# Where tiles of a shared PSUM ring stand beside a grouped-product unit, in a message-passing kernel on one core

## The chip, the cores and the metric

The kernel runs on one core of a Trainium2 chip. The metric is the device time of one execution in microseconds (us); lower is better. The engines are named as in the profile: PE (matrix products; PEld are its weight loads), DVE (vector engine), ACT (scalar engine), POOL (GpSimd) and SP, whose queue issues most DMAs.

## The reference

Cut to what matters (200000 edges, 6250 nodes, 128 features, 20 edge attributes):

```python
h = relu(layernorm(x)) @ W_in                                  # 6250 x 128
W_ij = (ssp(f_ij @ W_f1 + b_f1) @ W_f2 + b_f2) * cutoff        # 200000 x 128
out = segment_sum(h[idx_j] * W_ij, idx_i, num_segments=6250)   # scatter-add over the edges
return x + ssp(out @ W_o1 + b_o1) @ W_o2 + b_o2                # ssp(v) = softplus(v) - log 2
```

`idx_j` (dst) is sorted, and is drawn as 6250 times the square of a uniform number; `idx_i` (src) is random. So the gather walks slowly through the table of nodes, and the sum scatters to all of it.

## The kernel before

Edges are taken in chunks of 128 and quads of 512; there are 391 quads (`NQ`), and two quads make one load (`load_sc`). One long Python loop over iterations `i` writes the order of every engine by hand (`tc.manual_schedule`), as a pipeline in software: iteration `i` loads ahead, computes the first layer of quad `i` (tiles `z`, `e`, one-hot `oh`, then the guard `a`, L314), gathers and multiplies quad `i-1` (`xg`, `W`, `xc`, then the product `m`, L344), and sums and scatters quad `i-2`.

Sums over equal source nodes go two ways.

- A *plain* quad builds an equality matrix of its 128 source ids for each chunk (`s1_eq`, tile `eq`, L308, one iteration after its one-hot), multiplies with it on PE (`s3_pe`, tile `pp`, L356), copies (ACT, L364), and POOL scatters four chunks with an indirect DMA into one of four accumulators in DRAM (L399).
- A *sorted* quad (144 of them, `mpq` = 5, 8, 10, 13, 16, 18, ..., three in every 8 iterations) is permuted on chip instead: a rank of each edge within its group of nodes, one-hots `pm` (L484), products `pq` (L508), copies `mst` (L516). Each six sorted quads make a round, and a round is summed into the accumulator `accT` in SBUF in four **grouped-product units**. A unit has six one-hots on DVE (`unit_oh`, tile `so`, L583, one iteration ahead), 72 products on PE into four PSUM tiles (`unit_pe`, tiles `un`, L598), and four additions on DVE (`unit_evac`, L607 in the first round, else L609, one iteration later). There are 96 units. Up to the last four they stand in iterations 23, 26, 31, 34, 39, 42, ...: where `i` modulo 8 is 7 or 2.

Besides, `rank_group`, `rank_count` (PSUM tile `rkp`), `rank_own`, `rank_over` (`rko`) and `rank_slot` rank eight sorted quads at a time (18 groups); `prep_*` fills the node table for 256 nodes at a time (PSUM tiles `hps`, `xps`, to iteration 217); `over_row` and `over_sum` (`orow`, `osum`) gather the edges that overflow a group; `r0_load`, `r0_tp`, `r0_add` (`r0t`, `rtp`) add the first DRAM accumulator to `accT` in 13 pieces once it is complete, from iteration 373 on; `late_bias` (`bps`) folds two biases once.

There are two PSUM rings of four banks. The first, "A", holds `z`, `xg` and `W`. The second, "B", holds all the rest: `pp`, `pq`, `po`, `un`, `rkp`, `rko`, `orow`, `osum`, `hps`, `xps`, `rtp`, `bps`. Tiles take the banks of a ring in turn, so a tile waits for the last reader of the one four places ahead of it. A unit takes all four banks at once, and its products go round over the four tiles.

The order of one iteration (each `run` carries out what was put at that point; in a point, what was registered first goes first: prep, bias, `r0`, ranks, the sorted quads' own steps, units):

```python
run(i, "L"); run(i, "A0"); run(i, "D0")      # loads; ACT copies; DVE reads of last iteration's tiles
s3_idx(i - 3); s1_oh(i); s1_eq(i - 1)        # DVE
run(i, "D1")                                 # DVE
s2_pe_x(i - 1); s2_pe_w(i - 1); s1_pe(i + 1) # PE: xg, W, z
s1_exp(i); s1_ln(i); run(i, "A1"); s2_copy(i - 1)   # ACT
s1_guard(i); s2_m(i - 1)                     # DVE: a (L314), m or pt (L344)
s3_pe(i - 2); s3_copy(i - 2, 0); s3_copy(i - 2, 1)  # PE pp; ACT s
run(i, "PE2"); run(i, "A2"); run(i, "D2")    # PE: ring B; ACT; DVE: pm, so, pt
s3_scatter(i - 3); run(i, "S")               # POOL
```

In the iteration of a unit, `i-2` is a sorted quad and no `pq` or `po` is due, so PE's part of ring B holds the unit alone, with what else was put at "PE2" ahead of it. The buffers of tag `pm` (two) serve both the one-hots `pm` and the tiles `r0t`. After the loop comes a tail of 13 groups: it loads the other three accumulators from DRAM, adds `accT`, and applies the last two layers.

Of the kernel before, what the change touches and what calls it, by code (L numbers as in the profile page):

```python
# [30 lines left out]
RND = 6  # L31
RKQ = 8
PW = 386
PREP_GAP = 9
# [8 lines left out]
def tile_gnn(ctx: ExitStack, tc: tile.TileContext, x, fB, cT, srcT, srcr, dstr, win_, wf1, wf2, bias, bo1c, wo1,  # L43
# [11 lines left out]
    spread = big(NSC)  # L55
    NCH = -(-n_edges // P)
    NQ = -(-NCH // 4)
# [3 lines left out]
    NG = len(groups)  # L61
# [6 lines left out]
    GN = NP // GRP  # L68
    mpq = sorted_quads(NQ)
    mpi = {q: n for n, q in enumerate(mpq)}  # L70
    plain = {q: n for n, q in enumerate(q for q in range(NQ) if q not in mpi)}
    scat = [0] * (NQ + 12)
    for q in range(NQ):
        if q not in mpi:
            scat[q + 3] += min(4, NCH - 4 * q)
    for q in mpq[1::2]:
        scat[q + 9] += 1
    RET = max(120, sum(scat) - 64)
    ret_at = min(i for i in range(len(scat)) if sum(scat[:i + 1]) >= RET)

# [177 lines left out]
    def load_sc(s):  # L258
        n = min(SC, NQ * SEG - s * SC)
        pp, hh, nh = s % HALF, s // HALF, n // SEG  # L260
        top = caps[s]
        ft = fts[s % len(fts)]
        b, o = s * SC // BE, s * SC % BE
        nc.sync.dma_start(ft[:KF, :n], fsd[b].rearrange("g (r e) -> (g r) e", r=RB)[:, o:o + n])
        sb = ld.tile([P, SC], I16, tag="sb", name="sb")
        nc.sync.dma_start(sb[:, :n], src16[s:s + 1, :n].to_broadcast([P, n]))
        rb = ld.tile([NR, SC], BF16, tag="rb", name="rb")
        nc.sync.dma_start(rb[:, :n], reld[s:s + 1, :n].to_broadcast([NR, n]))
        wn = ld.tile([NR, 2, P], BF16, tag="wn", name="wn")
        _, regs = nc.values_load_multi_w_load_instructions(  # L270
            base_i[pp:pp + 1, hh, 0:nh], engines=[SP], min_val=0, max_val=top,
            skip_runtime_bounds_check_because="clamped on the chip to [0, top]")
        for j in range(nh):
            nc.sync.dma_start(wn[:, j, :], tab[bass.ds(regs[j] * 3, NR), :])
        loads[s] = (ft, sb, rb, wn)

    def s1_pe(q):
        ft = loads[q // 2][0]
        j = q % 2
        z = ps.tile([P, 512], F32, tag="A", name="z", bufs=4)  # L280
        nc.tensor.matmul(z, ws, ft[:K1, j * SEG:(j + 1) * SEG], start=True, stop=True)  # L281
        st.setdefault(q, {})["z"] = z
# [12 lines left out]
    def s1_oh(q):  # L295
        rb = loads[q // 2][2]
        j = q % 2
        oh = wk.tile([NR, 512], BF16, tag="oh", name="oh")
        nc.vector.tensor_scalar(oh, rb[:, j * SEG:(j + 1) * SEG], rowid[:NR], None, op0=ALU.is_equal)  # L299
# [342 lines left out]
    with tc.manual_schedule():  # L642
# [107 lines left out]
        def at(i, point, fn, *a):  # L750
            hooks.setdefault((i, point), []).append((fn, a))

        def run(i, point):
            for fn, a in hooks.pop((i, point), []):
                fn(*a)
# [57 lines left out]
            at(t0 + 1, "A1", fb_3, b)  # L813
            at(t0 + 1, "D2", fb_4, b)

        mid = NQ // 6 * 3 if spread else 0

        def late_loads():
            nc.sync.dma_start(bo2b, bias[1:2, :].to_broadcast([P, P]))
# [43 lines left out]
        for t in range(0, NPT, 4):  # L863
            i = mid + 8 * (t // 4) if spread else 0
            at(min(i + 9, NQ + 1), "D2", x_bias, t)
        for g in range(len(tgroups)):
            i = ret_at + 3 + g
            at(min(i, NQ + 2), "L", r0_load, g)
            at(min(i + 2, NQ + 3), "PE2", r0_tp, g)
            at(min(i + 3, NQ + 4), "D0", r0_add, g)  # L870
        for r in range(-(-len(mpq) // RKQ)):
            i = mpq[RKQ * r]
            at(i - 4, "D2", rank_group, r)
            at(i - 3, "PE2", rank_count, r)
            at(i - 2, "D0", rank_own, r)
            at(i - 1, "PE2", rank_over, r)
            at(i, "D0", rank_slot, r)
        for q in mpq:
            at(q + 1, "D2", perm_oh, q)
            at(q + 2, "D2", part_rem, q, 1)  # L880
            at(q + 2, "D2", part_rem, q, 2)
            for s in range(4):
                at(q + 3 + s // 2, "PE2", permute, q, s)
                at(q + 4 + s // 2, "A0", perm_out, q, s)
            at(q + 4, "D1", perm_loc, q, 0)
            at(q + 5, "D1", perm_loc, q, 1)
            at(q + 4, "PE2", over_pe, q)
            at(q + 5, "A0", over_out, q)
            if mpi[q] % 2:
                at(q + 5, "D2", over_idx, q)  # L890
                at(q + 6, "PE2", over_row, q)
                at(q + 7, "D0", over_eq, q)
                at(q + 8, "PE2", over_sum, q)
                at(q + 9, "A0", over_copy, q)
                at(q + 9, "D1", over_ji, q)
                at(q + 9, "S", over_scatter, q)
        last = mpq[-1]
        for r in range(len(mpq) // RND):
            nxt = [mpq[n] + 2 for n in range(RND * (r + 1), min(RND * (r + 2), len(mpq))) if mpq[n] - mpq[n - 1] == 3]
            for s in range(4):  # L900
                k = nxt[s] if nxt else last + 6 + 2 * s
# [5 lines left out]
        for i in range(max(NQ + 6, last + 14)):  # L907
# [12 lines left out]
            if 0 <= i - 1 < NQ:  # L920
                s2_pe_x(i - 1)
                s2_pe_w(i - 1)
            if i + 1 < NQ:
                s1_pe(i + 1)
            if i < NQ:
                s1_exp(i)
                s1_ln(i)
            run(i, "A1")
            if 0 <= i - 1 < NQ:
                s2_copy(i - 1)  # L930
            if i < NQ:
# [12 lines left out]
            run(i, "S")  # L944
# [17 lines left out]
    with tc.For_i(0, trips, 1) as ci:  # L962
# [47 lines left out]
        s = wk.tile([P, P], F32, bufs=1, tag="dg", name="fs")  # L1010
# [112 lines left out]
def sorted_quads(nq):  # L1123
    qs, q = [], MP0
    while q < nq - MPEND:
        qs.append(q)
        q += MPGAPS[(len(qs) - 1) % len(MPGAPS)]
    return qs[:len(qs) // RND * RND]


def runs(qs):
# [109 lines left out]
```

## Time and profile before

| | |
|---|---|
| runs | 2337.44, 2331.75, 2336.96 us; median 2336.96 us |
| profiled execution | 2332.85 us; its span, first to last instruction, 2331.0 us |
| mean granted TensorE clock | 0.948 |
| busy, share of the span | PE 86%, DVE 84%, POOL 74%, ACT 73% |
| last scatter issued | 2272.3 us, then the tail |

A row of the profile's groups reads: line, engine, operation, tiles written <- read, times it occurs | busy us, mean ns of one | idle time of the engine just before it, and what ended most of that. A row of the waits reads: who waited <- for whom: us in total, times, longest. A row of the timeline reads: start, duration (several alike merged, xN), and in brackets the idle time before it and what ended that. A row of the windows gives a stretch, its length, each engine's busy time, and the granted clock.

### The profile page before, as it was taken

How to read it: one execution, taken by the hardware profiler on the slowest of the kernel's cores; microseconds unless marked ns; L12 is line 12 of the kernel's file. 1: busy time of each engine (PE TensorE's matmuls, PEld its weight loads, DVE VectorE, ACT ScalarE, POOL GpSimd, SP SyncE). 2: the span in 40 equal slices, each digit the busy share in tenths (PEclk: the TensorE clock that was granted, in tenths of full speed). 3: DMA queues.
4: the chain of work that ended last, by engine and by line, in shares of the span. 5: the costliest groups of instructions: out<-in, count | busy, mean ns of one | idle time of the engine just before them, and what ended most of it. 6: DMA issues, size and time to landing. Idle time of an engine off the chain costs nothing.

```text
span 2331.0 us, 55463 instructions
## 1 busy us (share of the span) xinstructions
PE 2009.1 (86%) x19201; PEld 1405.5 (60%) x19201; DVE 1946.9 (84%) x5586; ACT 1706.7 (73%) x4286; POOL 1728.0 (74%) x1101
## 2 busy tenths in 40 slices
PE   4878988888889888989898989898989898987775
PEld 3556655666656565656565656665666565664543
DVE  6778988888889888879898989898989898886565
ACT  4777877786778776868787878786878787875534
POOL 3678778776768676768677888787878787886464
PEclk8899999999999999999999999999999999998888
DMA  8977768676767676767766767776767676776438
GB/s 295 246 167 138 155 126 164 118 154 119 152 126 157 136 145 121 148 136 144 146 136 140 160 119 157 143 148 130 150 136 148 137 156 121 148 154 136 98 34 223
DMA packets 391004, 341.76 MB, mean 147 GB/s; under 512 B 86760, under 2 KB 305742, under 8 KB 390720
## 3 DMA queue, kind: packets, MB, share of 16 engines
q1 hardware_dynamic: 237136, 265.37, 38.0%
q0 software_dynamic: 153296, 72.75, 32.0%
q8 instruction: 151, 2.47, 0.4%
q14 instruction: 133, 1.09, 0.2%
q10 hardware_dynamic: 288, 0.07, 0.0%
HBM read 198.15 MB, written 139.90 MB: 145 GB/s over the span
## 4 chain that ended last, share of the span: by engine, by line
PE 45%; DVE 30%; ACT 11%; DMA 6%; issue 5%; SPq 1%; POOL 1%; DVEq 0%; ACTq 0%; POOLq 0%
PE pq L508 10%; PE un L598 10%; PE W L333 8%; PE pp L356 6%; DMA acc<-s,ji 4%; DVE so L583 4%; DVE pm L484 4%; ACT xc L339 3%; DVE pt L498 3%; DVE a L314 3%; PE W L330 2%; PE xg L325 2%; DVE eq L308 2%; DVE m L344 2%; ACT e L287 2%
## 5 line engine op out<-in xcount | busy, mean ns | idle before, releaser
L399 POOL DMA_INDIRECT acc<-s,ji x987 | 1573.9, 1595 | 526.4 <-issue 170.5
L339 ACT ACTIVATE xc<-xg,cT_sb 128x128 f32<-128x128 f32 x1564 | 440.4, 362 | 268.0 <-PE xg L325 258.7
L598 PE MATMUL un<-so,mst 32*128 32x392 bf16 x6912 | 381.1, 365 | 186.2 <-DVE pr L448 56.6
L508 PE MATMUL pq<-pt,pm 128*128 128x386 bf16 x2304 | 452.5, 335 | 27.7 <-ACT s L364 15.2
L333 PE MATMUL W<-w,a 128*128 128x128 f32 x3128 | 460.4, 291 | 0.0
L333 PEld LDWEIGHTS W<-w,a 128*128 128x128 f32 x3128 | 385.0, 194 | 95.7 <-issue 95.3
L598 PEld LDWEIGHTS <-mst 32*128 32x128 bf16 x6912 | 206.8, 103 | 344.4 <-issue 159.4
L516 ACT CAST mst<-pq 128x386 bf16<-128x386 f32 x576 | 271.8, 500 | 95.9 <-PE pq L508 79.5
L508 PEld LDWEIGHTS <-pm 128*128 128x128 bf16 x2304 | 223.5, 98 | 180.5 <-issue 37.7
L314 DVE SCALAR_TENSOR_TENSOR a<-z,e 128x512 f32<-128x512 f32 x391 | 267.4, 684 | 70.4 <-ACT e L292 43.4
L292 ACT ACTIVATE e<-e,con 128x512 f32<-128x512 f32 x391 | 282.2, 722 | 12.7
L609 DVE TENSOR_TENSOR accT<-un,accT 128x392 f32<-128x392 f32 x368 | 182.2, 557 | 125.8 <-PE un L598 113.1
L356 PEld LDWEIGHTS pp<-m,eq 128*128 128x128 f32 x1976 | 262.3, 194 | 37.0 <-DVE accT L609 24.6
L356 PE MATMUL pp<-m,eq 128*128 128x129 f32 x1976 | 268.9, 280 | 16.8 <-DVE accT L609 15.2
L364 ACT COPY s<-pp 128x258 f32<-128x258 f32 x494 | 172.9, 391 | 115.8 <-PE pp L356 75.6
L287 ACT ACTIVATE e<-e 128x512 f32<-128x512 f32 x391 | 246.6, 631 | 12.4
L286 ACT ACTIVATE e<-z 128x512 f32<-128x512 f32 x391 | 236.5, 605 | 9.9 <-PE z L281 8.2
L484 DVE TENSOR_SCALAR pm<-iot,pos 128x576 bf16<-128x576 f16 x576 | 187.3, 387 | 19.8 <-PE rtp L845 7.3
L498 DVE TENSOR_TENSOR pt<-pt 128x512 f32<-128x512 f32 x288 | 198.6, 689 | 0.0
L344 DVE TENSOR_TENSOR m<-W,xc 128x512 f32<-128x512 f32 x247 | 168.3, 681 | 13.1 <-ACT xc L339 6.2
L325 PE MATMUL xg<-wn,oh 126*128 126x128 bf16 x1564 | 155.4, 222 | 16.2 <-DVE oh L299 7.5
L308 DVE TENSOR_TENSOR eq<-sb,srcT_sb 128x512 f32<-128x512 int16 x247 | 168.6, 682 | 0.0
(156 smaller groups left out, 2649.9 us busy)
## 6 DMA issues: line engine op xcount, KB each, us to landing
sb<-src SPq DMA_DIRECT2D x195, 256.0 KB
rb<-reld SPq DMA_DIRECT2D x195, 252.0 KB
ft<-fsd SPq DMA_DIRECT2D x195, 240.0 KB
fsd<-f SPq DMA_DIRECT2D x49, 480.0 KB
acc<-s,ji POOLq DMA_INDIRECT x987
fb<-in_fB_dram SPq DMA_DIRECT2D x49, 320.0 KB
fsd<-f SPq DMA_DIRECT2D x49, 320.0 KB
wn<-tab SPq DMA_DIRECT2D x391, 31.5 KB
```

Of the source, the lines that this page charges most:

```text
L287: nc.scalar.activation(e, e, AF.Exp, scale=-1.0)
L292: nc.scalar.activation(e, e, AF.Ln, bias=half, scale=0.5)
L314: nc.vector.scalar_tensor_tensor(a, st[q]["z"], 0.0, st[q]["l"], op0=ALU.max, op1=ALU.add)
L333: nc.tensor.matmul(W[:, c, :], st[q]["a"][:, c * P:(c + 1) * P], w2, start=False, stop=(c == 3))
L339: nc.scalar.mul(xc[:, c, :], st[q]["xg"][:, c, :], cT_sb[:, 4 * q + c:4 * q + c + 1])
L356: nc.tensor.matmul(pp[:, c, :129], st[q]["eq"][:, k, :], m[:, k, :129], start=True, stop=True)
L399: nc.gpsimd.indirect_dma_start(out=accs[k][:, :], out_offset=bass.IndirectOffsetOnAxis(ap=ji, axis=0), in_=s, in_offset=None, compute_op=A ...
L484: nc.vector.tensor_scalar(pm[:, c], iot[:, :SLOTS], rk[r]["pos"][:, 4 * j + c:4 * j + c + 1], None, op0=ALU.is_equal)
L498: nc.vector.tensor_tensor(pt[:, :, k * P:(k + 1) * P], a, high(a), op=ALU.subtract)
L508: nc.tensor.matmul(t[:, :PW], mp[q]["pm"][:, c, s * P:(s + 1) * P], high(mp[q]["pt"][:, c:c + 1, :PW])[:, 0], start=(c == 0), stop=(c == 3))
L516: nc.scalar.copy(mp[q]["ms", a][:, b], mp[q].pop(("q", s))[:, :PW])
L598: nc.tensor.matmul(ts[g][:, :GN], mp[q]["ms", s // 2][v, s % 2, k * P:(k + 1) * P], mp[q]["oh"][v], start=(q == qs[0] and k == 0), stop=(q ...
```

## The change

1. **Tiles of ring B that DVE reads an iteration later leave the units' iterations.** `clear(i, units)` gives the first iteration from `i` on without a unit. `rkp` and its start `rank_group` come one iteration earlier than before, `rko` in the next iteration that has no unit, and `rank_slot` behind that. Groups of `prep_*` are put off by up to two iterations so that neither `hps` nor `xps` meets a unit, with their loads, their DVE and ACT steps and their write to the table. The `rtp` pieces skip the units' iterations and each stands behind the last one, from 376 to 391 (before: 375 to 387), their loads two iterations ahead. `osum` and one `orow` move one iteration on (ACT reads `osum`); with `osum` go its copy, its index and its scatter on POOL. `late_bias` moves from iteration 201 to 200.
2. **A unit's additions follow the equality matrix.** `unit_evac` goes from point "D0" of the iteration behind the unit to "D1": behind `s3_idx`, `s1_oh` and `s1_eq`.

Of the 96 units, 26 shared their iteration with a tile that DVE reads an iteration later: `rkp` (11), `rko` (6), `xps` (6) or `rtp` (4), one of them with two. Some 24 shared it with `osum` and five with `hps`, which ACT reads. After the change none shares it with any of these. No engine has more or fewer instructions: PE, DVE, ACT, POOL and SP have as many rows in the program's order as before.

The diff, cut to its core:

```diff
+    units = unit_its(mpq)
...
     for q in mpq[1::2]:
-        scat[q + 9] += 1
+        scat[q + 10] += 1
...
-        mid = NQ // 6 * 3 if spread else 0
+        busy = units | {prep_start(g) + k for g in range(1, NG) for k in range(5)}
+        mid = clear(NQ // 2, busy, 2) - 6 if spread else 0
...
         for g in range(len(tgroups)):
-            i = ret_at + 3 + g
-            at(min(i, NQ + 2), "L", r0_load, g)
-            at(min(i + 2, NQ + 3), "PE2", r0_tp, g)
-            at(min(i + 3, NQ + 4), "D0", r0_add, g)
+            i = clear(max(r0_at + 1, ret_at + 5), units)
+            r0_at = i
+            at(i - 2, "L", r0_load, g)
+            at(i, "PE2", r0_tp, g)
+            at(i + 1, "D0", r0_add, g)
...
-            at(i - 4, "D2", rank_group, r)
-            at(i - 3, "PE2", rank_count, r)
-            at(i - 2, "D0", rank_own, r)
-            at(i - 1, "PE2", rank_over, r)
-            at(i, "D0", rank_slot, r)
+            at(i - 5, "D2", rank_group, r)
+            k = clear(i - 4, units)
+            at(k, "PE2", rank_count, r)
+            at(k + 1, "D0", rank_own, r)
+            k = clear(k + 1, units)
+            at(k, "PE2", rank_over, r)
+            at(k + 1, "D0", rank_slot, r)
...
-                at(q + 6, "PE2", over_row, q)
-                at(q + 7, "D0", over_eq, q)
-                at(q + 8, "PE2", over_sum, q)
-                at(q + 9, "A0", over_copy, q)
...
+                k = clear(q + 6, units)
+                at(k, "PE2", over_row, q)
+                at(k + 1, "D0", over_eq, q)
+                k = clear(q + 8, units)
+                at(k, "PE2", over_sum, q)
+                at(k + 1, "A0", over_copy, q)
...
                 at(k - 1, "D2", unit_oh, r, s)
                 at(k, "PE2", unit_pe, r, s)
-                at(k + 1, "D0", unit_evac, r, s)
+                at(k + 1, "D1", unit_evac, r, s)
...
+def clear(i, busy, n=1):
+    while any(i + k in busy for k in range(n)):
+        i += 1
+    return i
...
 def prep_start(g):
-    return 6 + PREP_GAP * (g - 1)
+    busy = unit_its(sorted_quads(4 * PREP_GAP * (g + 8)))
+    return clear(7 + PREP_GAP * (g - 1), busy, 2) - 1
```

PE, around the ranks of quads 282 on. Before, the rank's tile `rkp` stands in iteration 279, right ahead of that iteration's unit:

```order
L281 LDWEIGHTS ws
L281 MATMUL z<-ft_117,ws 128x512
L433 LDWEIGHTS tri
L433 MATMUL rkp<-G,tri 128x512
L437 LDWEIGHTS onesb
L437 MATMUL rkp<-G,onesb 128x8x48
L437 LDWEIGHTS onesb
L437 MATMUL rkp<-G,onesb 128x8x32
L437 LDWEIGHTS onesb
L437 MATMUL rkp<-G,onesb 128x8x16
L598 LDWEIGHTS mst
L598 MATMUL un<-so,mst 128x392
```

In the changed program, on PE, the same ranks stand in iteration 278, ahead of that iteration's two `pq` and one `po`:

```order
L434 LDWEIGHTS tri
L434 MATMUL rkp<-G,tri 128x512
L438 LDWEIGHTS onesb
L438 MATMUL rkp<-G,onesb 128x8x48
L438 LDWEIGHTS onesb
L438 MATMUL rkp<-G,onesb 128x8x32
L438 LDWEIGHTS onesb
L438 MATMUL rkp<-G,onesb 128x8x16
L509 LDWEIGHTS pm
L509 MATMUL pq<-pt,pm 128x386
```

Of ring B's four banks, the unit's fourth tile took the one that `rkp` held; now three tiles stand between, and the unit's first tile takes it.

DVE, at the same unit. Before, the rank's reading (L448 to L453) and the four additions stand together at the start of iteration 280, and the one-hot and the equality matrix behind them:

```order
L498 TENSOR_TENSOR pt<-pt 128x4x128
L448 TENSOR_TENSOR pr<-rkp,G 128x512
L451 TENSOR_REDUCE rank<-pr 128x32
L453 TENSOR_SCALAR ov<-rank 128x32
L609 TENSOR_TENSOR accT<-un,accT 128x392 x4
L299 TENSOR_SCALAR oh<-rb,con 126x512
L308 TENSOR_TENSOR eq<-sb,srcT_sb 128x512
L314 SCALAR_TENSOR_TENSOR a<-z,e 128x512
```

In the changed program, DVE at the start of iteration 280:

```order
L499 TENSOR_TENSOR pt<-pt 128x4x128
L300 TENSOR_SCALAR oh<-rb,con 126x512
L309 TENSOR_TENSOR eq<-sb,srcT_sb 128x512
L610 TENSOR_TENSOR accT<-un,accT 128x392 x4
L315 SCALAR_TENSOR_TENSOR a<-z,e 128x512
```

and at the start of iteration 279, behind the unit's one-hots:

```order
L584 TENSOR_SCALAR so<-iot,lo 128x392 x6
L449 TENSOR_TENSOR pr<-rkp,G 128x512
L452 TENSOR_REDUCE rank<-pr 128x32
L454 TENSOR_SCALAR ov<-rank 128x32
L380 SCALAR_TENSOR_TENSOR jf<-s,con,jd 128x4
```

The reading of the rank moved an iteration ahead, and the additions moved behind the equality matrix.

More of the change, by code (lines that the diff above doesn't have):

```diff
@@ L865, in tile_gnn @@
             at(min(i + 9, NQ + 1), "D2", x_bias, t)
+        r0_at = 0
         for g in range(len(tgroups)):
-            i = ret_at + 3 + g
-            at(min(i, NQ + 2), "L", r0_load, g)
-            at(min(i + 2, NQ + 3), "PE2", r0_tp, g)
-            at(min(i + 3, NQ + 4), "D0", r0_add, g)
+            i = clear(max(r0_at + 1, ret_at + 5), units)
[3 more added lines that the diff above has]
+            at(i + 1, "D0", r0_add, g)
         for r in range(-(-len(mpq) // RKQ)):
             i = mpq[RKQ * r]
-            at(i - 4, "D2", rank_group, r)
-            at(i - 3, "PE2", rank_count, r)
-            at(i - 2, "D0", rank_own, r)
-            at(i - 1, "PE2", rank_over, r)
-            at(i, "D0", rank_slot, r)
+            at(i - 5, "D2", rank_group, r)
[5 more added lines that the diff above has]
+            at(k + 1, "D0", rank_slot, r)
         for q in mpq:
@@ L890, in tile_gnn @@
                 at(q + 5, "D2", over_idx, q)
-                at(q + 6, "PE2", over_row, q)
-                at(q + 7, "D0", over_eq, q)
-                at(q + 8, "PE2", over_sum, q)
-                at(q + 9, "A0", over_copy, q)
-                at(q + 9, "D1", over_ji, q)
-                at(q + 9, "S", over_scatter, q)
+                k = clear(q + 6, units)
[4 more added lines that the diff above has]
+                at(k + 1, "A0", over_copy, q)
+                at(k + 1, "D1", over_ji, q)
+                at(k + 1, "S", over_scatter, q)
         last = mpq[-1]
         for r in range(len(mpq) // RND):
-            nxt = [mpq[n] + 2 for n in range(RND * (r + 1), min(RND * (r + 2), len(mpq))) if mpq[n] - mpq[n - 1] == 3]
-            for s in range(4):
-                k = nxt[s] if nxt else last + 6 + 2 * s
+            for s, k in enumerate(unit_slots(mpq, r)):
                 at(k - 1, "D2", unit_oh, r, s)
                 at(k, "PE2", unit_pe, r, s)
-                at(k + 1, "D0", unit_evac, r, s)
+                at(k + 1, "D1", unit_evac, r, s)
+        r0_end = r0_at
         s1_pe(0)
-        for i in range(max(NQ + 6, last + 14)):
+        for i in range(max(NQ + 6, last + 14, r0_end + 2)):
             if i % 2 == 0 and i // 2 + 2 <= (NQ - 1) // 2:
@@ L1128, in sorted_quads, with unit_slots, unit_its @@
     return qs[:len(qs) // RND * RND]
+def unit_slots(qs, r):
+    nxt = [qs[n] + 2 for n in range(RND * (r + 1), min(RND * (r + 2), len(qs))) if qs[n] - qs[n - 1] == 3]
+    return nxt[:4] if nxt else [qs[-1] + 6 + 2 * s for s in range(4)]
+def unit_its(qs):
+    return {i for r in range(len(qs) // RND) for i in unit_slots(qs, r)}
+def clear(i, busy, n=1):
+    while any(i + k in busy for k in range(n)):
+        i += 1
+    return i
 def runs(qs):
```

## The prediction

> **What bounds the kernel now.** First the page: how busy each engine is, and what its largest groups wait for.
>
> ```profile
> PE 2009.1 (86%) x19201; PEld 1405.5 (60%) x19201; DVE 1946.9 (84%) x5586; ACT 1706.7 (73%) x4286; POOL 1728.0 (74%) x1101
> L399 POOL DMA_INDIRECT acc<-s,ji x987 | 1573.9, 1595 | 526.4 <-issue 170.5
> ```
>
> No engine is full over the span. The scatters on POOL look idle for 526.4 us, but each is followed by a fixed pause (the 0.30 in the timeline below), so I return to them. Second, the waits, for who stops whom at a unit.
>
> ```profile
> ACT xc L339 <- PE xg L325: 258.7, 53, 11.4
> DVE accT L609 <- PE un L598: 113.1, 26, 5.8
> PE un L598 <- DVE pr L448: 56.6, 10, 6.9
> PE un L598 <- DVE rm L211: 23.3, 7, 5.4
> PE un L598 <- DVE accT L852: 22.7, 7, 6.0
> DVE accT L609 <- PE xg L325: 9.5, 2, 5.1
> DVE accT L607 <- PE un L598: 8.3, 2, 4.8
> ```
>
> DVE's additions wait for the unit, and the unit's products wait for DVE steps (`pr` of `rkp`, `rm` of `xps`, `accT` of L852 of `rtp`) that read just the tiles that shared ring B with it. Third, the timeline of one such unit, iteration 279:
>
> ```profile
> 1597.68 1.46 DVE L583 TENSOR_SCALAR so<-iot,lo 128x392 bf16<-128x392 f16 x6
> 1598.05 0.34 PE L598 MATMUL un<-so,mst 32*128 32x392 bf16 x3 [0.83 <-DVE so L583]
> 1603.30 0.68 DVE L448 TENSOR_TENSOR pr<-rkp,G 128x512 f32<-128x512 f32 x1
> 1604.03 5.40 PE L598 MATMUL un<-so,mst 32*128 32x392 bf16 x69 [5.65 <-DVE pr L448]
> 1608.07 1.54 POOL L399 DMA_INDIRECT acc<-s,ji  x1 [0.30 <-issue]
> 1609.35 1.98 DVE L609 TENSOR_TENSOR accT<-un,accT 128x392 f32<-128x392 f32 x4 [4.44 <-PE un L598]
> ```
>
> Three products run; the fourth is the first into the bank that `rkp` holds, and waits 5.65 us until DVE, a whole iteration behind, has read `rkp`. Then it is DVE that stands 4.44 us for the unit. The two engines take turns where they should overlap. Fourth, windows of the same eight iterations' length (273 to 280 with this unit against 265 to 272 without), and the unit alone against a free one (iteration 295):
>
> ```profile
> core 0: us, PE busy (x) PEld busy (x) DVE busy (x) ACT busy (x) POOL busy (x), PEclk, DMA share, GB/s
> 1525.57:1564.70 39.13, 37.67 (x387) 27.00 (x385) 36.15 (x99) 33.46 (x86) 33.03 (x21) 1.00 0.76 155
> 1564.70:1612.80 48.10, 40.44 (x388) 27.83 (x387) 40.51 (x114) 33.47 (x84) 39.88 (x26) 0.93 0.69 132
> 1598.40:1609.50 11.10, 5.47 (x72) 3.00 (x72) 6.52 (x20) 2.13 (x4) 9.53 (x6) 0.69 0.41 37
> 1685.80:1689.10 3.30, 3.30 (x75) 1.87 (x75) 3.23 (x11) 3.24 (x8) 2.24 (x2) 1.00 0.24 35
> ```
>
> The stretch with it is 8.97 us longer. DVE has 40.51 - 36.15 = 4.36 us more work there (the ranks); the other 4.61 us is about the 4.44 us wait. In the free stretch PE (37.67 of 39.13) and DVE (36.15) are nearly full: work or waits of DVE there show in full. The unit after a wait also runs at a granted clock of 0.69, not 1.00: 5.40 us for 69 products against 3.16 us for 72.
>
> **The change part by part.** No instruction is added or removed; only waits can change.
>
> *(a) Waits of DVE for a held-up unit.* They are 113.1 + 9.5 + 8.3 = 130.9 us. The last four units are not in the loop's pace:
>
> ```profile
> DVE accT L609 <- PE un L598: 12.1, 4, 3.6
> 2272.32 1.62 POOL L399 DMA_INDIRECT acc<-os,oji  x1 [0.31 <-DVE so L583]
> 2282.41 1.26 POOL L1036 TENSOR_TENSOR ta_in<-ta_in 128x512 f32<-128x512 f32 x1 [8.47 <-DMA ta_in<-acc]
> ```
>
> (the first row from the waits after 2245 us). The tail's first sum waits for transfers that follow the last scatter, so the 12.1 us there stay and cost nothing. That leaves 118.8 us, all at the 26 units that share ring B with `rkp`, `rko`, `xps` or `rtp`. With those tiles gone from the units' iterations the fourth tile waits for nothing, PE does its 3.16 us while DVE does its iteration, and DVE need not wait. By the 4.61 us against 4.44 us above, a wait removed is time removed: **-118.8 us**. Bounds: 0, were another engine to set the pace at once; 131 were the end to gain too.
>
> *(b) The stretch of the first accumulator, from 2110 us.* `r0t` and the one-hots `pm` share two buffers, so DVE waits there for PE's transposes:
>
> ```profile
>   PE rtp L845: 7.3, 2
>   PE po L532: 5.4, 1
>   DMA ft<-fsd: 3.9, 1
>   PE W L333: 3.2, 1
> ```
>
> 19.8 us in five places (what `pm` waited for). The pieces now start later and skip units. Following the two buffers through the new order, only the `pm` of quads 378 and 386 wait for a transpose an iteration ahead, where it was five. I take half: **-10 us** (0 to -20). Each `r0_load` waits on SP's queue for its buffer, with `load_sc` of later quads behind it; those are fetched two iterations or more ahead, so I cost that at nothing. If it fails, a wait like the 3.9 us for `ft` comes back.
>
> *(c) Additions behind the equality matrix.* Nothing waits for DVE's one-hot or matrix at that place, while PE waits for the additions, which free the ring. Two free units, at `i` modulo 8 = 2 and 7:
>
> ```profile
> 1667.00 1.97 DVE L609 TENSOR_TENSOR accT<-un,accT 128x392 f32<-128x392 f32 x4
> 1668.89 0.46 DVE L299 TENSOR_SCALAR oh<-rb,con 126x512 bf16<-126x512 bf16 x1
> 1669.27 0.67 DVE L314 SCALAR_TENSOR_TENSOR a<-z,e 128x512 f32<-128x512 f32 x1
> 1667.61 1.19 PE L356 MATMUL pp<-m,eq 128*128 128x129 f32 x8 [0.98 <-DVE pt L498]
> 1690.10 1.98 DVE L609 TENSOR_TENSOR accT<-un,accT 128x392 f32<-128x392 f32 x4
> 1691.99 0.34 DVE L299 TENSOR_SCALAR oh<-rb,con 126x512 bf16<-126x512 bf16 x1
> 1692.85 0.68 DVE L314 SCALAR_TENSOR_TENSOR a<-z,e 128x512 f32<-128x512 f32 x1
> 1692.13 1.54 PE L508 MATMUL pq<-pt,pm 128*128 128x386 bf16 x8
> 1658.48 0.69 DVE L344 TENSOR_TENSOR pt<-W,xc 128x512 f32<-128x512 f32 x1 [0.96 <-PE pq L508]
> ```
>
> At 1667.61 `pp` already waits 0.98 us, and starts just as the first addition ends (1667.00 + 0.56). There the additions move behind the one-hot alone (the quad is a sorted one and has no matrix): 1669.27 - 1668.89 = 0.38 us later. At 1692.13 `pq` takes the fourth bank as the fourth addition ends (1692.08); there they move by 1692.85 - 1691.99 = 0.86 us. And PE's lateness comes round: `pq` is copied by ACT ahead of `e` and `xc`, for which DVE waits (1658.48, 0.96 us). Passed on in full that is 1.24 us in each 8 iterations, times 48 pairs of units: 60 us. At nothing it would be 0. I take two thirds, **+40 us**: 18 of the 48 stretches carry a rank's 4.36 us on DVE, which fill such waits. What is queued behind the additions (`a`, `m`) starts no later, since the order among one-hot, matrix and additions leaves their sum as it was.
>
> *(d) `rkp` an iteration ahead.* In 11 of the 18 groups, and three times for `rtp`, the tile now stands in the iteration just ahead of a unit, and by the ring's turn the unit's *first* tile takes its bank. So no product starts until DVE, done with the six `so`, has read it (`pr`, 0.68 us). The nearest rows: at iteration 279 the first products came 0.83 us late for the first `so`; now it is five more `so` (5/6 of 1.46 us) and `pr`, or some 2 us later. DVE then has its iteration ahead (in the old order from the end of `so` at 1599.14 to `pr` at 1603.30, 4.2 us) and the 0.86 us of (c), against a unit of 3.16 to 5.40 us. So it mostly hides; without that cover each unit would show its 2 us. **+5 us** (0 to 14 x 2 = 28).
>
> By the trace a pause near that length can cost speed as well:
>
> ```profile
> 1003.30 4.82 PE L598 MATMUL un<-so,mst 32*128 32x392 bf16 x69 [2.32 <-DVE rm L211]
> ```
>
> After 2.32 us idle (0.82 us more shortly before) the 69 products took 4.82 us. The Trainium skill, "TensorE: Matmul & The Clock Gate", Part 1, has the clock halve only after an idle window of about 3.4 us; by that the pauses of (d) would cost no clock, by the row they may cost 1.7 us each of PE's time, 14 x 1.7 = 24 us at most, which lies in the 28 above. I keep the row.
>
> *(e) The rest* moves whole: `prep_*` with its load and table write on SP (the gather reads node 6250(i/391)^2 at iteration i, far behind the table's 256 nodes per nine iterations), `osum` with copy, index and one POOL scatter, `late_bias`. POOL's scatters are as many as before, and the last moved one still queues behind those of the last plain quads. 0 us; should the table be late, a gather would wait some us once.
>
> Sum: -118.8 - 10 + 40 + 5 = -84 us, on the profiled 2332.85 us: 2249 us. The median of the runs is 4 us above that execution, so **2253 us**.
>
> **The rivals.**
>
> *A. The additions' new place costs nothing.* Then -129 + 5: about 2213 us. For it: rank stretches, and early ones, have DVE as the last to come. Against: the 0.98 us and 0.96 us waits above, which make a closed chain in the free stretches.
>
> *B. The scatters take over.* In the free stretch POOL has 33.03 us in 21 scatters and 21 x 0.30 us of pauses: 39.3 us of 39.13. It is full, and stays full in the stretch with the held-up unit (39.88 + 26 x 0.30 = 47.7 of 48.10), because it works off what has queued. Over the program, with
>
> ```profile
> L399 POOL DMA_INDIRECT acc<-os,oji x72 | 118.2, 1641 | 30.2 <-DVE a L314 8.6 <-issue 7.6 <-ACT e L292 2.4
> ```
>
> its idle time beyond the pauses is 526.4 + 30.2 - 1059 x 0.30 = 239 us, of which part lies ahead of the first scatter. So on the whole there is room for 84 us, but little in the second half. If what is left there holds the loop, half of (a), 59 us, is lost: about 2312 us. The Trainium skill, "SBUF — State Buffer", says that descriptors written by GpSimd stall while DVE holds a port the two share; no row here separates that, and the scatters' 1.54 to 1.82 us would be its bound.
>
> *C. Slower.* The later additions let PE go cold in the turn behind every unit. Price: a turn of PE at half clock loses about 1.7 us (a 3.4 us turn from 1667.61 to 1671), times 96 units, 163 us, with the 60 us of (c) against -129: 2337 + 94 = 2431 us. It decides from a wait of some 2.3 us per unit (the row above); the waits seen are 0.98 us and would grow to 1.3, so I hold it unlikely.
>
> *D. It does not do what it says:* the units' waits only move to their first tile (d) and DVE waits as long. Against: DVE's 4.2 us of other work between. It would stay near 2335 us.
>
> **How the numbers follow.** Forecast (waits go, the additions cost 20 to 60 us): 0.60, 2225 to 2280 us. A: 0.15, to 2205. B: 0.19, 2280 to 2325. C: 0.03. D: 0.03. The range 2205 to 2302 leaves out C, D, half of B and the far ends: 0.2. A measurement of this kernel tells about 0.3% (7 us) from no change. Faster: the forecast, A, B: 0.94; same: D, 0.03; slower: C, 0.03.
>
> **What would show it.** (a) the waits of L610 for `un` fall from 131 to under 25 us, those of `xc` for `xg` from 258.7 to under 80, the mean clock rises from 0.948 to 0.97 or more. (b) `pm`'s waits fall to about 10 us. (c) `pp` and `pq` wait longer for `accT`: from 39.8 us (24.6 + 15.2 below) to 70 or more, and a free stretch of eight iterations takes 40 us or more instead of 39.1.
>
> ```profile
> PEld pp L356 <- DVE accT L609: 24.6, 26, 2.6
> PE pp L356 <- DVE accT L609: 15.2, 17, 2.2
> ```
>
> (d) `un` waits for `pr` some 2 us at 11 units. I am wrong if free stretches stay at 39.1 us (A), or if POOL has no pause above 0.3 us from 500 us on (B).

## The result, and the profile after

| | before | after |
|---|---|---|
| runs | 2330.51 to 2337.44 us (4), median 2334.36 | 2242.91 to 2245.81 us (4), median 2244.53 |
| profiled execution, its span | 2332.85 us, 2331.0 us | 2243.32 us, 2241.2 us |
| mean granted TensorE clock | 0.948 | 0.968 |

The ratio is 0.9616 [0.9596, 0.9635]: faster by some 90 us (0.0384 x 2334). The forecast was 2253 us.

The page of the changed kernel: busy shares, then two groups (line, engine, operation, tiles, count | busy us, mean ns | idle before it and what ended most of it).

```profile
PE 1999.5 (89%) x19201; PEld 1396.4 (62%) x19201; DVE 1952.6 (87%) x5586; ACT 1712.1 (76%) x4286; POOL 1728.9 (77%) x1101
L400 POOL DMA_INDIRECT acc<-s,ji x987 | 1577.6, 1598 | 441.1 <-issue 177.8
L599 PE MATMUL un<-so,mst 32*128 32x392 bf16 x6912 | 318.6, 328 | 32.2 <-DVE so L584 11.3
```

The work is the same: busy times of all engines are within 1% of before. Only idle time went: the scatters' from 526.4 us to 441.1, and the units' products now stand idle for 32.2 us in all, against 186.2 us before, 56.6 of them for `pr`. The waits of the changed kernel (who <- for whom: us in total, times, longest):

```profile
ACT s L365 <- PE pp L357: 210.3, 120, 6.1
PEld pp L357 <- DVE accT L610: 111.7, 85, 3.5
DVE a L315 <- ACT e L293: 96.5, 86, 3.9
PE pp L357 <- DVE accT L610: 78.4, 69, 3.1
ACT xc L340 <- PE xg L326: 29.4, 45, 2.1
DVE pm L485 <- PE po L533: 17.3, 6, 6.9
DVE accT L610 <- PE un L599: 13.7, 4, 4.8
PE un L599 <- DVE pr L449: 10.6, 10, 1.3
```

Two families can be read side by side. The old one has nearly gone: the additions wait for the unit 13.7 us in four places (113.1 in 26 before), `xc` waits for `xg` 29.4 us (258.7). A new one has come: `pp` waits for the additions 111.7 + 78.4 = 190.1 us (39.8 before), ACT's copy waits for `pp` 210.3 us (75.6 before), and DVE's guard `a` waits 96.5 us for ACT's `e` (43.4 before on this line of `e`, and 17.2 on another).

The timeline at the unit shown before, iteration 279 (start, duration, what; in brackets the idle time before it and who ended it):

```profile
1555.06 0.34 PE L599 MATMUL un<-so,mst 32*128 32x392 bf16 x3
1555.12 0.68 DVE L449 TENSOR_TENSOR pr<-rkp,G 128x512 f32<-128x512 f32 x1
1555.86 3.14 PE L599 MATMUL un<-so,mst 32*128 32x392 bf16 x69 [0.46 <-DVE pr L449]
1561.75 1.98 DVE L610 TENSOR_TENSOR accT<-un,accT 128x392 f32<-128x392 f32 x4
1562.36 1.19 PE L357 MATMUL pp<-m,eq 128*128 128x129 f32 x8 [1.41 <-DVE accT L610]
```

The unit's pause for `pr` is 0.46 us where it was 5.65; its 69 products take 3.14 us where they took 5.40; and the additions start with no idle time ahead of them, 2.75 us after the last product (1555.86 + 3.14 = 1559.00). The price stands in the last row: `pp` waits 1.41 us for the first addition.

Windows of eight iterations, a free stretch (264 to 272) and the one with this unit (272 to 280) (columns as before: stretch, length, busy time with count of PE, PEld, DVE, ACT, POOL, granted clock, DMA share, GB/s):

```profile
1481.57:1521.66 40.09, 38.57 (x388) 26.64 (x387) 35.54 (x98) 33.82 (x85) 33.39 (x21) 1.00 0.74 151
1521.66:1564.32 42.66, 39.11 (x394) 27.35 (x393) 40.19 (x115) 34.01 (x84) 35.12 (x22) 1.00 0.71 143
```

The stretch with the ranks went from 48.10 us to 42.66, at a clock of 1.00; the free stretch grew from 39.13 to 40.09. So the change gains in some places and loses in others, as foretold; the runs below separate the parts.

### The profile page after: what moved, and what is told of

Read it like the earlier page. It is cut to its first block, busy times and chain, and to the rows that moved or that the text cites. A ratio compares the mean times of both kernels' runs of the same rounds, so it can differ in the third digit from the quotient of the medians.

```text
span 2241.2 us, 55463 instructions
## 1 busy us (share of the span) xinstructions
PE 1999.5 (89%) x19201; PEld 1396.4 (62%) x19201; DVE 1952.6 (87%) x5586; ACT 1712.1 (76%) x4286; POOL 1728.9 (77%) x1101
## 5 line engine op out<-in xcount | busy, mean ns | idle before, releaser
L400 POOL DMA_INDIRECT acc<-s,ji x987 | 1577.6, 1598 | 441.1 <-issue 177.8
L509 PE MATMUL pq<-pt,pm 128*128 128x386 bf16 x2304 | 464.2, 341 | 20.4 <-ACT s L365 16.1
L340 ACT ACTIVATE xc<-xg,cT_sb 128x128 f32<-128x128 f32 x1564 | 441.6, 363 | 33.3 <-PE xg L326 29.4
L357 PE MATMUL pp<-m,eq 128*128 128x129 f32 x1976 | 286.0, 290 | 83.9 <-DVE accT L610 78.4
L315 DVE SCALAR_TENSOR_TENSOR a<-z,e 128x512 f32<-128x512 f32 x391 | 266.6, 682 | 96.7 <-ACT e L293 96.5
L599 PE MATMUL un<-so,mst 32*128 32x392 bf16 x6912 | 318.6, 328 | 32.2 <-DVE so L584 11.3
L357 PEld LDWEIGHTS pp<-m,eq 128*128 128x128 f32 x1976 | 267.8, 200 | 125.3 <-DVE accT L610 111.7
L365 ACT COPY s<-pp 128x258 f32<-128x258 f32 x494 | 174.0, 391 | 223.0 <-PE pp L357 210.3
L599 PEld LDWEIGHTS <-mst 32*128 32x128 bf16 x6912 | 184.5, 94 | 159.6 <-issue 38.5
L485 DVE TENSOR_SCALAR pm<-iot,pos 128x576 bf16<-128x576 f16 x576 | 188.5, 388 | 17.3 <-PE po L533 17.3
L610 DVE TENSOR_TENSOR accT<-un,accT 128x392 f32<-128x392 f32 x368 | 181.4, 552 | 15.4 <-PE un L599 13.7
```

Source lines behind the costliest of these rows:

```text
L315: nc.vector.scalar_tensor_tensor(a, st[q]["z"], 0.0, st[q]["l"], op0=ALU.max, op1=ALU.add)
L340: nc.scalar.mul(xc[:, c, :], st[q]["xg"][:, c, :], cT_sb[:, 4 * q + c:4 * q + c + 1])
L357: nc.tensor.matmul(pp[:, c, :129], st[q]["eq"][:, k, :], m[:, k, :129], start=True, stop=True)
L400: nc.gpsimd.indirect_dma_start(out=accs[k][:, :], out_offset=bass.IndirectOffsetOnAxis(ap=ji, axis=0), in_=s, in_offset=None, compute_op=A ...
L509: nc.tensor.matmul(t[:, :PW], mp[q]["pm"][:, c, s * P:(s + 1) * P], high(mp[q]["pt"][:, c:c + 1, :PW])[:, 0], start=(c == 0), stop=(c == 3))
L599: nc.tensor.matmul(ts[g][:, :GN], mp[q]["ms", s // 2][v, s % 2, k * P:(k + 1) * P], mp[q]["oh"][v], start=(q == qs[0] and k == 0), stop=(q ...
```

## The experiments

Ratios are to the kernel before, timed in the same session. A cost in us is a difference of two ratios times 2337 us; an interval of about +-0.0016 on a ratio is +-4 us, and the difference of two such ratios is good to about +-6 us. Stretches of iterations are cut at the ends of the guards `a`.

**1. Additions first.** The changed kernel with the additions back ahead of the one-hot:

```diff
-                at(k + 1, "D1", unit_evac, r, s)
+                at(k + 1, "D0", unit_evac, r, s)
```

> The changed kernel with one thing undone: a unit's four additions stand at the start of the next iteration again, ahead of its one-hot and equality matrix; the tiles stay away from the units. Theory 1 (a held-up unit was a wait of DVE, and the additions' new place costs about 1 us per 8 iterations, since it frees ring B later): free stretches of 8 iterations go back from 40.1 to 39.1 us, the waits of pp for accT fall from 190 us (111.7 + 78.4) towards 40, and the time is 35 to 45 us under the changed kernel's 2244, near 2204 us. Theory 2 (the new place gives DVE work while the unit runs, and is part of the gain): DVE waits for un come back at the 11 units that have rkp an iteration ahead, 2250 us or more. Theory 3 (the scatters on POOL already set the pace): the loop gains less than 20 us, since POOL has only some 20 us of idle time beyond its pauses between 1300 and 2110 us; 2225 to 2240 us.

Measured: median 2205.48 us (2201.47 to 2212.36), ratio 0.9424 [0.9408, 0.9439]. The additions' new place costs (0.9616 - 0.9424) x 2337 = 45 us, about what its first theory said (near 2204 us). Its waits (the profiled execution is the longest of the four, 2212.36 us):

```profile
ACT s L365 <- PE pp L357: 129.5, 101, 4.7
PEld pp L357 <- DVE accT L610: 54.4, 47, 2.6
DVE a L315 <- ACT e L293: 51.0, 44, 4.2
PE pp L357 <- DVE accT L610: 36.9, 34, 2.3
```

and its free stretch at 264:

```profile
1461.45:1500.14 38.69, 37.56 (x385) 26.32 (x384) 35.97 (x99) 33.45 (x85) 32.59 (x21) 1.00 0.77 156
```

`pp`'s waits halve, and with them goes the rest of the chain: ACT's waits for `pp` fall by 80.8 us, DVE's on this line of `e` by 45.5. The free stretch loses 1.40 us. This is the fastest complete version, 2.0% under the changed kernel (0.9424 / 0.9616).

**2. The additions' move alone**, in the kernel before:

```diff
-                at(k + 1, "D0", unit_evac, r, s)
+                at(k + 1, "D1", unit_evac, r, s)
```

> The kernel before with the additions' move alone: behind the equality matrix, the tiles where they were. Theory 1: at the 26 held-up units DVE does its one-hot and matrix (0.38 or 0.86 us) while it would wait, which gains at most 26 x 0.6 = 16 us; the free stretches lose 1 us each, some 26 of 48: 10 us or more over the kernel before's 2334, near 2344 us. Theory 2 (the move is part of the gain): faster by 15 us or more, 2320 us or less.

Measured: 2371.55 us (2364.39 to 2375.82), ratio 1.0129 [1.011, 1.0148]: 30 us slower. The sign is as expected, the size three times that.

```profile
ACT xc L339 <- PE xg L325: 243.4, 57, 11.3
DVE accT L609 <- PE un L598: 90.8, 25, 5.6
```

By this row DVE waits 22.3 us less for held-up units (90.8 against 113.1), since the one-hot and the matrix fill the beginning of the wait, but that bought no time: the held-up stretch at 272 takes 48.13 us (48.10 before). `xc` waits for `xg` nearly as long as before (243.4 against 258.7); that this stops DVE next is likely, but not shown by itself. The free stretch at 264 takes 40.14 us, as in the changed kernel, not 39.13. The placing alone, with late additions, is worth (1.0129 - 0.9616) x 2337 = 120 us; with early additions (before against run 1) 135 us.

**3. The ranks put back** beside the units, all else as changed:

```diff
-            at(i - 5, "D2", rank_group, r)
-            k = clear(i - 4, units)
-            at(k, "PE2", rank_count, r)
-            at(k + 1, "D0", rank_own, r)
-            k = clear(k + 1, units)
-            at(k, "PE2", rank_over, r)
-            at(k + 1, "D0", rank_slot, r)
+            at(i - 4, "D2", rank_group, r)
+            at(i - 3, "PE2", rank_count, r)
+            at(i - 2, "D0", rank_own, r)
+            at(i - 1, "PE2", rank_over, r)
+            at(i, "D0", rank_slot, r)
```

> The changed kernel with the ranks (rkp, rko and their DVE steps) where they were before, all else as changed: 17 units are held up again. Theory 1: their waits of DVE come back, 45.7 us for rkp and 27.1 us for rko in the kernel before's trace, less 0.4 to 0.9 us each that DVE now fills with its one-hot and matrix: 55 to 65 us more than the changed kernel, 2300 to 2310 us. Theory 3 (POOL's queue takes up such waits): less than 30 us more, under 2275 us.

Measured: 2344.38 us (2340.96 to 2346.78), ratio 1.0021 [1.0011, 1.003]: the ranks' places are worth 95 us, more than any theory had said. DVE's own waits do not explain it:

```profile
ACT xc L340 <- PE xg L326: 161.1, 54, 11.1
DVE accT L610 <- PE un L599: 62.8, 18, 4.8
DVE accT L610 <- PE xg L326: 7.8, 2, 4.2
DVE accT L608 <- issue: 4.0, 1, 4.0
```

The last row is the unit of iteration 23, one of the 17 held up, though the view names no engine for it. The additions wait 62.8 + 7.8 + 4.0 = 74.6 us for units, only 60.9 above the 13.7 of the changed kernel, and 95 us go with it. The timeline of iterations 279 to 281 shows what else comes with such a wait (DVE, and ACT's row at 1639.60):

```profile
1639.44 1.99 DVE L610 TENSOR_TENSOR accT<-un,accT 128x392 f32<-128x392 f32 x4 [3.61 <-PE xg L326]
1639.60 1.14 ACT L340 ACTIVATE xc<-xg,cT_sb 128x128 f32<-128x128 f32 x4 [8.90 <-PE xg L326]
1645.93 0.69 DVE L315 SCALAR_TENSOR_TENSOR a<-z,e 128x512 f32<-128x512 f32 x1 [1.59 <-ACT e L293]
1647.59 0.69 DVE L345 TENSOR_TENSOR pt<-W,xc 128x512 f32<-128x512 f32 x1 [0.96 <-ACT xc L340]
```

DVE stands 3.61 us for the unit (the row puts it down to PE's `xg` next in line). ACT stood 8.90 us for the `xg` queued behind that unit, comes out of it late, and makes DVE wait another 1.59 and 0.96 us for `e` and `xc`. In the changed kernel, of these waits, only one of 0.96 us is left between 1546 and 1576 us. That the missing 34 us are such later waits is read from this one unit; they were not added up. The stretch from 272 to 280:

```profile
1593.62:1642.02 48.40, 40.22 (x389) 27.84 (x388) 40.74 (x115) 33.55 (x84) 39.23 (x25) 0.93 0.73 139
```

It takes 48.40 us; in the changed kernel 42.66: 5.74 us less, and 95 us over 17 units is 5.6 each. The 42.66 is 2.57 us over the free stretch's 40.09, though the ranks give DVE 4.65 us more work in it (40.19 against 35.54). With the hold-up gone, part of that work runs in time that DVE otherwise waits.

**4. The pieces of the first accumulator put back:**

```diff
-            i = clear(max(r0_at + 1, ret_at + 5), units)
-            r0_at = i
-            at(i - 2, "L", r0_load, g)
-            at(i, "PE2", r0_tp, g)
-            at(i + 1, "D0", r0_add, g)
+            i = ret_at + 3 + g
+            at(min(i, NQ + 2), "L", r0_load, g)
+            at(min(i + 2, NQ + 3), "PE2", r0_tp, g)
+            at(min(i + 3, NQ + 4), "D0", r0_add, g)
```

> The changed kernel with the 13 pieces of the first accumulator (r0t, rtp) where they were before: four units are held up again near the end. Theory 1: 21.4 us of DVE waits for un and some 10 us for pm come back: 20 to 30 us more than the changed kernel, 2265 to 2275 us, all of it between iterations 368 and 391. Theory 3: less than 10 us more, since the scatters still queued at the end of the loop set the tail's start.

Measured: 2272.68 us (2270.54 to 2273.91), ratio 0.9717 [0.9701, 0.9733]: 24 us. Its waits:

```profile
DVE accT L610 <- PE un L599: 31.7, 8, 5.5
DVE pm L485 <- PE rtp L847: 14.2, 4, 4.4
DVE pm L485 <- PE po L533: 6.6, 1, 6.6
```

The additions wait 31.7 - 13.7 = 18.0 us more, all at the four units near the end, and most of the 24. The buffers of `pm` matter little: 14.2 + 6.6 = 20.8 us of waits here, 17.3 in the changed kernel. The pieces still make `pm` wait there in the changed kernel.

**5. The node table's steps put back:**

```diff
-    busy = unit_its(sorted_quads(4 * PREP_GAP * (g + 8)))
-    return clear(7 + PREP_GAP * (g - 1), busy, 2) - 1
+    return 6 + PREP_GAP * (g - 1)
```

> The changed kernel with the groups of the node table (hps, xps) where they were before: six units are held up again, at iterations 26 to 215. Theory 1: their DVE waits for the unit come back, 9.5 + 15.1 us and a part of 3.4 us in the kernel before's trace, and as much again behind them, as at the ranks: 25 to 45 us more than the changed kernel's 2244, 2270 to 2290 us. Theory 3 (in the first 500 us the scatters queue up to 28 us deep in the changed kernel, and their pace takes up what the loop loses): only the units at 143, 170 and 215 show, 10 to 20 us more, 2254 to 2264 us.

Measured: 2256.04 us (2251.2 to 2257.24), ratio 0.9645 [0.9629, 0.9661]: about 7 us, with intervals that overlap (0.9635 and 0.9629). All expectations were higher. The waits came back as they should:

```profile
DVE accT L610 <- PE un L599: 36.4, 10, 5.6
DVE accT L608 <- PE un L599: 4.4, 1, 4.4
```

27.1 us more of DVE waiting (36.4 + 4.4 against 13.7), for 7 us of time. Two neighbouring stretches, 24 to 32 and 32 to 40, first with the steps put back:

```profile
162.02:208.30 46.28, 41.41 (x396) 28.46 (x395) 38.65 (x114) 34.76 (x88) 37.02 (x23) 0.96 0.74 141
208.30:250.81 42.51, 39.45 (x394) 27.64 (x393) 38.27 (x114) 34.87 (x89) 34.03 (x22) 1.00 0.76 150
```

and as changed:

```profile
162.09:205.17 43.08, 39.68 (x396) 27.50 (x395) 39.18 (x119) 34.99 (x90) 34.24 (x22) 1.00 0.77 149
205.17:249.89 44.72, 40.46 (x394) 28.60 (x393) 39.43 (x114) 34.91 (x89) 34.45 (x22) 0.96 0.74 145
```

The change gains 3.20 us in the first, where a unit was held up, and loses 2.21 us in the second, where none was. No group's steps came into the second: one group stands an iteration later in it (`xps` in 36, not 35), and the counts of instructions are nearly the same. DVE is busy 1.16 us longer there, and the clock is 0.96 where it was 1.00. Three more stretches without a held-up unit (from 72, 176 and 184) are 1.4 to 2.2 us longer as changed, and 1.4 to 2.4 us in run 4, which has the table's steps as changed too. Why they are stays open.

**6. Additions later still**, behind DVE's `m` or `pt`, at a new point "D3" after `s2_m`:

```diff
-                at(k + 1, "D1", unit_evac, r, s)
+                at(k + 1, "D3", unit_evac, r, s)
```

> The changed kernel with the additions put later once more, behind the guard a and the product m of their iteration (two steps of 0.60 us from start to start, 1.2 us per unit). Theory 1 (PE waits for ring B, and the wait goes round): the cost grows with the lateness: the first move, 0.38 or 0.86 us per unit, cost 39 to 45 us; 1.2 us more on each of 96 units costs 70 to 115 us, 2315 to 2360 us. Theory 4 (only the order against the one-hot counts, since PE needs it for xg): less than 20 us more, under 2264 us.

Measured: 2386.59 us (2383.52 to 2387.58), ratio 1.0204 [1.0189, 1.022]: 137 us over the changed kernel, above the 70 to 115 expected, and 1.4 us for each of 96 units, more than the 1.2 us by which the additions were to move.

```profile
PEld pp L357 <- DVE accT L610: 213.5, 88, 4.5
PE pp L357 <- DVE accT L610: 179.3, 88, 4.1
DVE a L315 <- ACT e L293: 159.5, 113, 3.7
```

At three places of the additions, `pp`'s waits for them are 91.3 (run 1), 190.1 and 392.8 us, and the median times 2205, 2245 and 2387 us. From the first step to the second 0.4 us of time go with each microsecond of `pp`'s waits, from the second to the third 0.7. A slack that is used up would explain that; it was not shown.

**7. Fewer scatters**: run 1 with three scatters for each plain quad instead of four.

```diff
-            scat[q + 3] += min(4, NCH - 4 * q)
+            scat[q + 3] += min(3, NCH - 4 * q)
...
-        for c in range(nchunks(q)):
+        for c in range(min(3, nchunks(q))):
```

> The variant with the additions first, with the fourth of the four scatters of each plain quad left out (some 247 of 1059; the sums lack those edges). It frees POOL of some 460 us. Theory 1 (the loop is paced by PE, ACT and DVE): the stretches of 8 iterations from 224 to 376 take as long as with all scatters, within 5 us in all; the time falls by the first 150 us, where the scatters queue, and at the tail, 10 to 25 us in all: 2180 to 2195 us. Theory 3 (POOL sets the pace by now): those stretches shorten by 20 us or more, 2160 us or less.

Measured: 2187.34 us (2186.78 to 2188.86), ratio 0.9356 [0.9341, 0.937], 16 us under run 1. A free stretch (264 to 272) and the stretch from iteration 224 to 368, in this run:

```profile
1442.02:1480.73 38.71, 37.64 (x385) 26.37 (x384) 35.71 (x98) 33.35 (x85) 26.48 (x17) 1.00 0.73 151
1236.96:1968.30 731.34, 697.96 (x7008) 486.77 (x7007) 679.11 (x1930) 609.00 (x1522) 471.87 (x297) 1.00 0.68 143
```

and the latter in run 1:

```profile
1255.69:1990.00 734.31, 701.29 (x7007) 490.47 (x7006) 684.94 (x1930) 609.89 (x1522) 612.48 (x381) 0.99 0.75 150
```

With 84 fewer instructions and 141 us less work on POOL (471.87 against 612.48) the loop takes 3 us less there, and the free stretch is as long as in run 1 (38.71 and 38.69). POOL does not set the pace of the second half, though its sum in run 1's free stretch, 32.59 + 21 x 0.30 = 38.89 of 38.69 us (the window shown there), reads as full. The expectation named the stretch to 376; its last eight iterations took 51.71 us here and 40.45 in run 1, because the pieces of the first accumulator start some seven iterations earlier when there are fewer scatters (`rtp` from 369 on, not 376), so they say nothing about POOL. The rest of the gain lies ahead of iteration 224: the first 32 iterations take 173.7 us against 181.4.

**8. Half the additions an iteration earlier**: run 1, with the additions of units at `i` modulo 8 = 2 at a new point "DE" ahead of "D2" of the unit's own iteration, save where `rkp` stands just ahead of the unit.

```diff
-                at(k + 1, "D0", unit_evac, r, s)
+                early = k % 8 == 2 and k < last and (k - 1, "PE2") not in ranked
+                at(k if early else k + 1, "DE" if early else "D0", unit_evac, r, s)
```

> The variant with the additions first, and at the units where i modulo 8 is 2 they stand earlier still: in the unit's own iteration behind its product m, ahead of the splits of pt (1.47 us), but not where rkp stands an iteration ahead. Theory 1: the unit has ended by then (un ended 2.2 us or more ahead of the additions there), so DVE waits for nothing, and the 0.98 us that pp waits for the first addition at each of some 40 such units goes: 20 to 40 us under 2205, 2165 to 2185 us. Theory 3 (POOL, with 10 us idle beyond its pauses from 1300 to 2110 us, holds the loop): less than 10 us gained, 2195 to 2205 us.

Measured: 2206.07 us (2200.88 to 2208.95), ratio 0.9436 [0.942, 0.9451]: the same as run 1, where a gain was expected.

```profile
PE pq L509 <- DVE pt L499: 30.6, 42, 1.5
PEld pp L357 <- DVE accT L610: 21.4, 22, 2.4
PE pp L357 <- DVE accT L610: 13.9, 14, 2.0
```

`pp`'s waits did fall, from 91.3 us to 35.3. What took their place stands in the timeline of the stretch from 264 (38.72 us long, 38.69 in run 1):

```profile
1467.23 1.97 DVE L610 TENSOR_TENSOR accT<-un,accT 128x392 f32<-128x392 f32 x4
1469.12 0.68 DVE L499 TENSOR_TENSOR pt<-pt 128x512 f32<-128x512 f32 x1
1470.58 1.54 PE L509 MATMUL pq<-pt,pm 128*128 128x386 bf16 x8 [0.77 <-DVE pt L499]
```

The early additions push the splitting of `pt` back, and `pq` waits 0.77 us for that; over the program it waits 30.6 us for `pt`, where run 1 has 0.7. One wait was traded for another. What holds the free stretch at 38.7 us is not POOL (run 7), and cutting `pp`'s waits did not shorten it. PE itself is busy for 37.29 us of it; no run takes work from PE, so whether PE is the bound stays open.

## Why the prediction was right

It was right in the time and in the two large terms. Some smaller terms missed, and the parts of the largest did not cost what their waits said; that these errors offset each other is luck.

**(a) DVE's waits for held-up units, -118.8 us.** Right as a sum. The placing alone is worth 120 us (run 2 against the changed kernel), where (a), (b) and (d) together said 124. Two of the three signs named for it came: waits of L610 for `un` under 25 us (13.7, all in the last four units), `xc` for `xg` under 80 (29.4). The clock came to 0.968, just short of 0.97. But "a wait removed is time removed" fails for the parts. A microsecond of DVE's wait for a unit was worth 1.6 us at the ranks (95 / 60.9, run 3), 1.3 at the pieces of the accumulator (24 / 18.0, run 4) and 0.3 at the node table (7 / 27.1, run 5; with the noise, 0 to 0.5). At the ranks the later wait for ACT, which stood for the same unit, had been left out. The rule had been read from one stretch, and held roughly on the mean (126 us of time for 106 of waits), because the rule gave too little at the ranks and too much at the table.

**(b) The buffers of `pm`, -10 us.** Mis-sized. Their waits fell from 19.8 us only to 17.3. The two quads that it named, 378 and 386, do wait, but for 5.7 and 6.9 us, which is most of that; the move of the pieces gains by its units, which (a) had counted.

**(c) Additions behind the matrix, +40 us.** Right: 45 us (run 1), inside the bounds of 0 and 60. Both signs came: `pp` waits 190.1 us for the additions (70 or more foretold), and the free stretch takes 40.09 us (40 or more). Its reason for less than the full 60 holds as well: from 224 to 368 the seven stretches that carry ranks lose 0.3 us on the mean against run 1, the other eleven 1.0. The loop it named, `pp`'s lateness to ACT and from ACT back to DVE, is seen in run 1, where the three waits fall together.

**(d) `rkp` an iteration ahead, +5 us.** At the right units, smaller than said, and not by the turn it gave: `un` waits for `pr` in ten places, 1.1 us on the mean, 1.3 at most, where some 2 us at 11 units were foretold. In all ten the first three products run and the fourth waits (the row at 1555.06 shows one), so it is still the unit's fourth tile that takes the bank of `rkp`, not its first: the banks of the ring do not go strictly in turn, as was said. DVE's iteration of cover held: the additions do not wait there. What it costs was not timed by itself, but it cost no clock: behind all ten pauses the 69 products took 3.14 us. The Trainium skill, "TensorE: Matmul & The Clock Gate", Part 1, puts the idle window that halves the clock at about 3.4 us. The ten pauses agree with that; the row that the prediction kept, a pause of 2.32 us in the kernel before, does not, as the granted clock around it was 0.79:

```profile
1000.00:1008.20 8.20, 5.22 (x73) 2.91 (x73) 3.49 (x9) 2.45 (x6) 6.97 (x5) 0.79 0.64 114
```

**(e) The rest at 0 us.** Mis-sized for `prep_*`: four stretches without a held-up unit grew by 1.4 to 2.2 us each, which gave back part of what the new place saved; why they grew is open (run 5). The moves of `osum`, one `orow` and `late_bias` were not tried alone. The parts that were, -95 - 24 - 7 + 45 = -81 us of the 90, leave them and what the parts do to each other some 9 us, within the noise of four such differences.

**The rivals.** A (the additions' place is free, 2213 us) falls by the free stretches and run 1; its time is nearly that of run 1, the version without their move. B (the scatters take over) falls: POOL's idle time beyond its pauses, by the prediction's sum, fell from 239 us to 441.1 + 22.5 - 1059 x 0.30 = 146 and did not stop the gain; pauses above 0.3 us are left (1.35 us at 1554.72 below), and run 7 shows no pace set by POOL in the second half. The 22.5 us is from this row of the changed kernel's groups:

```profile
L400 POOL DMA_INDIRECT acc<-os,oji x72 | 114.9, 1596 | 22.5 <-issue 7.0 <-ACT e L288 2.4 <-ACT s L365 2.1
```

The rule weighed beside B, that of the Trainium skill's "SBUF — State Buffer", section "SBUF: two separate sides", on the port that DVE and GpSimd share, cannot be read from the means: 1598 ns with DVE busy for 87% of the span, and 1595 with 84%. The single scatters of the changed kernel do show that their time goes with what DVE does:

```profile
1554.72 1.90 POOL L400 DMA_INDIRECT acc<-s,ji  x1 [1.35 <-ACT e L287]
1560.62 1.76 POOL L400 DMA_INDIRECT acc<-s,ji  x1 [0.30 <-issue]
1564.54 1.54 POOL L400 DMA_INDIRECT acc<-s,ji  x1 [0.31 <-issue]
```

The first starts while DVE makes the one-hots `so`, the second while it splits `pt` in SBUF, the third while it multiplies from PSUM. The 125 scatters that start while DVE is idle take 1.54 us on the mean, and so do the 90 that start beside a unit's additions; the 110 that start while `pt` is split take 1.76. That is what a shared port would do, though no run changes it alone. Over the program the time beyond 1.54 us each is 1577.6 + 114.9 - 1059 x 1.54 = 62 us of POOL's time, and 61 us before, so it has no part in the gain.

C (PE goes cold) falls by the clock of 1.00 in the free stretches; D (the waits only move) by the 13.7 us.

## What to carry to other kernels

When a burst of products takes every bank of a ring at once, keep its iteration free of tiles that an engine with a fixed order of work reads an iteration later; here that was worth 120 of 2337 us with no work removed. Price such a hold-up by the length of one stretch with it and without it (48.40 against 42.66 us at the ranks, where 17 units were worth 5.6 us each), not by one engine's wait: the engine that waits first is held again by the others that stood in the same queue. And an edit that is a gain as a whole can carry a loss inside: time each part by itself, as the additions' move, which alone costs 30 us in the kernel before and 45 in the changed one.

## What was not expected

- A sum of busy time and fixed pauses that fills a stretch (POOL, 38.89 of 38.69 us) did not make POOL the bound: with 84 of its 381 instructions left out, 144 iterations took 731.3 us instead of 734.3.
- The stretch with the ranks, with DVE busy for 40.19 us against 35.54 in the free one, takes only 2.57 us longer once nothing is held up (40.19 of 42.66 us).
- The cost of a late reader grows faster than its lateness: 45 us for the first step of the additions (0.4 to 0.9 us each, by the rows before), 137 us for the next (about 1.2 us each).
